# A recurrent mixer and an expert layer on one core: loads, tables and normalisation of the first block laid out anew

## The chip, the cores and the metric

The kernel runs on one NeuronCore of a Trainium2 chip. Five engines work side by side, each through its own queue in program order: PE (TensorE, matrix multiplication), DVE (VectorE), ACT (ScalarE), POOL (GpSimd) and SP (SyncE, which only issues DMAs here; ACT and POOL issue DMAs as well). [...]an instruction that waits holds up everything queued behind it on its engine. The metric is the device time of one execution in microseconds (us), lower is better.

## The reference

Two residual layers on x of shape (4, 1024, 256), float32. The first is a linear attention with decay over 16 heads of 16 channels; the second routes each token to two of eight experts, with a capacity for each expert. Cut to what matters here:

```python
x = x + attn(layernorm(x));  x = x + moe(layernorm(x))

# attn, for layer-normed x
xx = shift_by_one_token(x) - x                # the first token of a sequence has zero before it
k = (x + xx * maa_k) @ Wk.T                   # likewise r, v, and g = gelu(...)
w = exp(-exp(time_decay)); u = time_faaaa     # one number per head
Wmat[i, j] = w ** (i - j - 1) where i > j, u on the diagonal, 0 above
y     = (r @ k.T * Wmat) @ v + r @ state * w ** i
state = w ** Q * state + (k * w ** (Q - 1 - j)) @ v
out   = groupnorm_per_head(y) * ln_w + ln_b;  out = (out * g) @ Wo.T

# moe, for layer-normed x
the two largest of softmax(x @ gate_w.T), with a capacity of 320 per expert and sequence
final = sum over the two of prob * (silu(h @ w1) * (h @ w3)) @ w2
```

## The kernel before

**Tiling.** There are four sequences (b) of 1024 tokens, each cut into four blocks (blk) of 256 tokens, and each block into two chunks of 128. The recurrence is taken in chunks of Q = 128. x comes in eight loads of 512 tokens, that is of four tiles of 128, so that one load serves two blocks. `front` prepares a block: norm, transposition, the four mixed inputs, the projections r, k, v, g. `chunk` does the scores of a chunk, multiplies them with the decay tables, and updates the state; `back` does the head norm, the gate and the output projection; `route` the gate of the experts; `expert` one expert's three products. These are generators, and a loop written out by hand at the end of the kernel advances them turn by turn, block n's chunks beside block n+1's front. Experts are slotted in from block 6 on.

**Order.** The order of instructions on each engine comes from a scheduler that follows the program by priority and readiness. `tc.issue_after(ins)` holds the instructions of a `with` block behind ins, and `tc.keep_in_program_order(ins)` pins one to its place. Tiles of a pool with the same tag share `bufs` buffers in turn: the writer of a tile waits for the last reader of the tile that had the buffer.

**The start.** These are the names and lines that matter:

- `ch` (L101): 14 columns for each of 128 partitions, holding the eight mixing weights, ln_w, ln_b and the decays by channel. `hd` (L103): the decay and the bonus u of each head, 2 x 16 numbers spread to all partitions by the DMA. `wa` (L105): the five 256 x 256 weights in one load of 1280 KB. `gt` (L112): the gate; `lw` (L114): ln_w over all partitions. ACT issues all five. SP issues the first load of x (L97).
- `nlam` and `nlam_c` (L186 to L190): -exp(decay) by head and by channel: an exponential on ACT and a step on DVE each.
- `dist` (L194, L196): max(i - j - 1, 0), made on POOL and cut at zero on DVE.
- `wb`, `wk`, `ws` (L204 to L206): decay tables for the state and the keys, exponentials on ACT; `wsb` (L207) is ws spread over 128 columns by DVE.
- `wmat` (L209): 16 exponentials on ACT, one 128 x 128 table per head, then one `affine_select` on POOL (L211) that clears what is not strictly earlier, then `diagonals` (L218): 16 steps on DVE that add u on the diagonal.
- `centre_values` (L177 to L179): DVE takes the mean per head out of Wv's columns, giving `wvc`.
- `norm_stats` (L275 to L279): statistics of all four tiles of a load on DVE, with the reciprocal root by three Newton steps; `normed` (L285) applies them on ACT, tile by tile, into `xn`.
- In `front`: column 0 of `xT`, the last token of the block before (L303 for a sequence's first block, L305 on DVE for the others); the transposes `trx` (L310); their copy to `xT` on ACT (L313); `xx` on POOL (L315); `mixed` (L320), two steps on DVE for each of k, r, v; the projections `pc` (L330); v's product `pt` with wvc (L362); `kT` (L346), `rT` (L351), `rbT` (L352, needs wb), `vpad` (L367), the transposes `pk` (L376) and `kw` (L380, needs wk); g's mixed input `xm_g` on POOL (L387, L390). `xm` has two buffers.
- In `chunk`: the scores `pa` (L403), their product with wmat, `aw`, on DVE (L409), y (L426), `pu` (L436), and `state` on POOL (L450, needs wsb).
- `empty` (L815): a tile of zeros with token numbers, from which SP clears the experts' input `disp` in 32 stores (L240). The first eight go out as soon as empty is ready; then comes the load of the second half of sequence 0's x, a store to the output, and the other 24.

The start-up calls before, as the scheduler gets them: fronts(0); one step of the front; then `centre_values` behind the last step of the norm; the fill of `empty`; the clears; two more steps of the front; then all diagonals behind the same norm step.

On ACT that gives this order: the loads, the table of functions, nlam, nlam_c, the first tile's xn, wb (2), wk, ws, wmat (16), the second tile's xn, the copy of xT.

Of the kernel before, what the change touches and what calls it, by code (L numbers as in the profile page):

```python
# [8 lines left out]
F32 = mybir.dt.float32  # L9
I32 = mybir.dt.int32  # L10
# [39 lines left out]
def rwkv_then_moe_kernel(  # L50
# [4 lines left out]
    head: bass.AP,  # L55
# [39 lines left out]
    def load_x(b, r):  # L95
        t = keep.tile([P, RT, C], F32, tag="x", name=f"x{b}_{r}", bufs=4)
        nc.sync.dma_start(out=t, in_=rows(x, b, r))  # L97
        xb[b, r] = t

    ch = const.tile([P, 14], F32, tag="ch", name="ch")  # L100
    nc.scalar.dma_start(out=ch, in_=chan)  # L101
    hd = const.tile([P, 2, H], F32, tag="hd", name="hd")
    nc.scalar.dma_start(out=hd, in_=head.partition_broadcast(P))  # L103
    wa = const.tile([P, 5, CC, C], F32, tag="wa", name="wa")
    nc.scalar.dma_start(  # L105
        out=wa.rearrange("p w cc d -> p (w cc) d"),
        in_=w_attn.rearrange("(k p) d -> p k d", p=P),
    )
# [3 lines left out]
    nc.scalar.dma_start(out=gt[:, :, :E], in_=gate.rearrange("(cc p) e -> p cc e", p=P))  # L112
    lw = const.tile([P, C], F32, tag="lw", name="lw")
    nc.scalar.dma_start(out=lw, in_=lnw.partition_broadcast(P))  # L114

    load_x(0, 0)
# [47 lines left out]
    empty = fp.tile([P, 2, EK, W], F32, tag="w", name="empty", bufs=5)  # L164
# [8 lines left out]
    def centre_values():  # L173

        wv = wa[:, W_V, :, :].rearrange("p cc (h n) -> p (cc h) n", n=N)
        vmean = const.tile([P, CC * H], F32, tag="vmean", name="vmean")
        tc.keep_in_program_order(nc.vector.tensor_reduce(vmean, wv, AX.X, ALU.add))  # L177
# [15 lines left out]
    dist = a1.tile([P, P], F32, tag="xx", name="dist")  # L193
    nc.gpsimd.iota(dist, pattern=[[1, P]], base=-1, channel_multiplier=-1,  # L194
                   allow_small_or_imprecise_dtypes=True)
    nc.vector.tensor_scalar_max(dist, dist, 0.0)  # L196
# [6 lines left out]
    for cc in range(CC):  # L203
        nc.scalar.activation(wb[:, cc, :], col, AF.Exp, scale=nlam_c[:, cc:cc + 1])  # L204
    nc.scalar.activation(wk, nlam, AF.Exp, scale=back_)
    nc.scalar.activation(ws, nlam_c, AF.Exp, scale=float(P))  # L206
    nc.vector.tensor_copy(wsb, ws.unsqueeze(2).to_broadcast([P, CC, P]))  # L207
    for h in range(H):
        nc.scalar.activation(wmat[:, h, :], dist, AF.Exp, scale=nlam[:, h:h + 1])  # L209

    nc.gpsimd.affine_select(  # L211
        out=wmat, in_=wmat, pattern=[[0, H], [1, P]], compare_op=ALU.is_gt, fill=0.0,
        base=0, channel_multiplier=-1,
    )

    def diagonals():
        for h in range(H):
# [72 lines left out]
    def front(b, blk, o):  # L290
# [4 lines left out]
        if h0 == 0:  # L295
            last["stats"] = norm_stats(src, f"a{nm}")
# [631 lines left out]
```

## Time and profile before

| | us |
|---|---|
| median of three runs | 1138.74 |
| lowest, highest | 1132.3, 1141.37 |
| the profiled execution: its time | 1138.5 |
| the same: span from the first to the last instruction | 1136.8 |
| first load of x issued; first statistics of it | 0.82; 4.87 |
| load of wa issued; first use of it that waited | 1.84; 10.37 |
| first clear issued on SP | 22.18 |
| first scores of block 0 on PE | 30.83 |

The mean granted clock of TensorE was 0.982 of full speed. By stretches of the profile: between 0 and 20 us PE is busy for 1.3 us, between 20 and 40 for 15.0, between 40 and 100 for 57.1 of 60, between 100 and 200 for 85.0 of 100, at a mean granted clock of 0.89, and from 200 to 1000 for 97% of the time.

A busy PE is not a PE at its peak: the matmuls are pipelined and their ends are modelled. What can be read off surely is when an engine stood idle, and the profile names for each such stretch what ended it. The times are from one execution.

### The profile page before, as it was taken

What the parts mean: (1) busy time and instruction counts of PE and PEld (TensorE: products, weight loads), DVE (VectorE), ACT (ScalarE), POOL (GpSimd) and SP (SyncE); (2) the same over time, 40 slices, a digit from 0 to 9 for tenths busy, and PEclk for the clock granted to TensorE, in tenths of its full rate; (3) what the DMA queues carried; (4) which work ended last, traced back from release to release, by engine and by line L of the source; (5) the groups of instructions that cost most, each with busy time, mean ns of one, the idle gap of its engine ahead of it and who ended that gap; (6) DMA issues with size and microseconds to landing.
All of it is one profiled execution on the core that took longest, in us unless ns stands there. A gap on an engine that the chain in (4) does not pass through costs nothing. (4 is left out here: it accounts for less than half of the span.)

```text
span 1136.8 us, 15008 instructions
## 1 busy us (share of the span) xinstructions
PE 1061.6 (93%) x5640; PEld 799.2 (70%) x5640; DVE 509.6 (45%) x1577; ACT 280.9 (25%) x561; POOL 273.9 (24%) x262
## 2 busy tenths in 40 slices
PE   2889997999999999999999999989999999999996
PEld 2556564677776777687778677778888766666664
DVE  4678775555455455637552745322222222222221
ACT  4324251423142324412341321311111111111110
POOL 3222243122312331233133213312121111111111
PEclk9999996999999999999999999999999999999998
DMA  4992011143523352254316245456565644444421
GB/s 122 241 291 75 16 61 39 57 117 100 162 60 104 124 148 84 52 155 135 103 29 206 69 117 164 150 151 202 163 185 178 175 129 132 130 121 130 126 47 16
DMA packets 91564, 138.24 MB, mean 122 GB/s; under 512 B 5600, under 2 KB 73056, under 8 KB 91488
## 3 DMA queue, kind: packets, MB, share of 16 engines
q1 hardware_dynamic: 76048, 117.63, 33.1%
q0 software_dynamic: 13440, 18.13, 9.1%
q10 hardware_dynamic: 2000, 1.47, 0.4%
q8 instruction: 47, 0.77, 0.3%
q14 instruction: 29, 0.24, 0.1%
HBM read 103.52 MB, written 33.69 MB: 121 GB/s over the span
## 5 line engine op out<-in xcount | busy, mean ns | idle before, releaser
L732 PE MATMUL p<-xeT,w 128*128 128x256 f32 (+1 forms) x1792 | 448.4, 407 | 2.2 <-DVE xeT L723 1.1
L732 PEld LDWEIGHTS p<-xeT,w 128*128 128x128 f32 x1792 | 337.9, 190 | 100.7 <-ACT sl L737 5.7
L755 POOL DMA_INDIRECT y_out<-ye,xe x72 | 115.4, 1603 | 514.6 <-DVE ye L753 454.2
L749 PE MATMUL pw<-w,act 128*128 128x256 f32 x1008 | 231.0, 383 | 6.9 <-DVE ye L753 4.9
L739 DVE TENSOR_TENSOR act<-sl,p 128x256 f32<-128x256 f32 (+1 forms) x224 | 101.5, 453 | 282.2 <-PE p L732 267.4
L749 PEld LDWEIGHTS pw<-w,act 128*128 128x128 f32 x1008 | 188.0, 191 | 42.7 <-DVE ye L753 6.5
L737 ACT ACTIVATE sl<-p 128x256 f32<-128x256 f32 (+1 forms) x224 | 90.7, 410 | 497.5 <-PE p L732 477.7
L753 DVE TENSOR_SCALAR ye<-pw,xe 128x256 f32<-128x256 f32 x72 | 34.8, 483 | 173.3 <-PE pw L749 152.0
L409 DVE TENSOR_TENSOR aw<-pa,wmat 128x512 f32<-128x512 f32 x128 | 84.7, 684 | 59.9 <-PE pa L403 54.7
L403 PE MATMUL pa<-rT,kT 64*128 64x512 f32 x256 | 90.9, 654 | 1.1 <-DVE aw L409 1.1
L658 POOL DMA_INDIRECT disp<-hs,is x64 | 62.5, 977 | 115.5 <-DVE hs L655 62.8
L330 PE MATMUL pc<-xm,wa 128*128 128x256 f32 x256 | 68.5, 412 | 15.8 <-DVE xm L320 15.8
L330 PEld LDWEIGHTS pc<-xm,wa 128*128 128x128 f32 x256 | 49.6, 205 | 31.5 <-issue 17.7
L426 PE MATMUL y<-aw,vpad 128*32 128x128 f32 x1024 | 49.6, 286 | 1.6 <-DVE aw L409 1.6
L451 POOL TENSOR_TENSOR state<-state,upd 128x256 f32<-128x256 f32 x24 | 18.4, 766 | 126.2 <-DVE upd L441 75.3
L320 DVE SCALAR_TENSOR_TENSOR xm<-xx,ch,xT 128x256 f32<-128x256 f32 x96 | 43.6, 477 | 10.6 <-PE pc L330 5.8
L351 ACT ACTIVATE rT<-pc,par 128x512 f32<-128x512 f32 x64 | 38.7, 688 | 39.0 <-PE pc L330 37.5
L426 PEld LDWEIGHTS y<-aw,vpad 128*32 128x32 f32 x1024 | 27.4, 111 | 19.6 <-issue 8.0
L403 PEld LDWEIGHTS pa<-rT,kT 64*128 64x128 f32 x256 | 25.2, 188 | 22.5 <-issue 16.2
L346 ACT COPY kT<-pc 128x512 f32<-128x512 f32 x16 | 9.4, 586 | 106.8 <-PE pc L330 106.8
L362 PE MATMUL pt<-wvc,xm 128*128 128x256 f32 x128 | 32.7, 400 | 1.0 <-DVE aw L409 1.0
L501 PE MATMUL po<-wa,zT 128*128 128x256 f32 x128 | 31.7, 390 | 1.6 <-DVE zT L493 1.6
(163 smaller groups left out, 882.0 us busy)
## 6 DMA issues: line engine op xcount, KB each, us to landing
w<-w_in SPq DMA_DIRECT2D x96, 896.0 KB, 5.2
disp<-empty SPq DMA_DIRECT2D x24, 265.0 KB, 9.6
xe<-disp SPq DMA_DIRECT2D x24, 265.0 KB, 2.8
disp<-empty SPq DMA_DIRECT2D x8, 530.0 KB, 14.6
x<-x_in SPq DMA_DIRECT2D x8, 512.0 KB, 3.6
y_out<-x SPq DMA_DIRECT2D x8, 512.0 KB, 3.4
xe<-disp SPq DMA_DIRECT2D x8, 397.5 KB, 3.2
wa<-w_attn_in ACTq DMA_DIRECT2D x1, 1280.0 KB
```

Of the source, the lines that this page charges most:

```text
L320: nc.vector.scalar_tensor_tensor(xm[:, cc, :], xx[:, cc, :], maa(m, cc), xT[:, cc, 1:TB + 1], ALU.mult, ALU.add,)
L330: nc.tensor.matmul(pp[:, m * TB:(m + 1) * TB], wa[:, w, cc, m * P:(m + 1) * P], xm[:, cc, :], start=cc == 0, stop=cc == CC - 1,)
L351: nc.scalar.activation(o.rT[:, :, q, :], pp, AF.Copy, scale=par[:, q:q + 1])
L403: nc.tensor.matmul(pa, o.kT[rows64, cc, cols], o.rT[rows64, cc, :, cols], start=True, stop=True, tile_position=(64 * g, 0),)
L409: nc.vector.tensor_tensor(w.rearrange("p q i -> p (q i)"), pa, wmat[:, h0:h0 + 4, :].rearrange("p q i -> p (q i)"), ALU.mult,)
L426: nc.tensor.matmul(y[32 * g:32 * g + 32, :], o.vp[:, t, cc * 4 + g, q * 32:(q + 1) * 32], aw[cc, g // 2][:, (g % 2) * 2 + q, :], start=sta ...
L658: ins = nc.gpsimd.indirect_dma_start(out=disp[:, :], out_offset=bass.IndirectOffsetOnAxis(ap=idx_s[b, r][:, k, t:t + 1], axis=0), in_=hs[: ...
L732: nc.tensor.matmul(pp[:, :w], wt[:, cc, f * P:(f + 1) * P], xeT[:, cc, :w], start=cc == 0, stop=cc == CC - 1,)
L737: nc.scalar.activation(sl[:, :w], p1[:, :w], AF.Silu)
L739: nc.vector.tensor_tensor(act[:, :w], sl[:, :w], p3[:, :w], ALU.mult)
L749: nc.tensor.matmul(po[:, o:o + C], acts[f][:, t * P:(t + 1) * P], w2e[:, f, :], start=f == 0, stop=f == FC - 1,)
L755: ins = nc.gpsimd.indirect_dma_start(out=out[:, :], out_offset=bass.IndirectOffsetOnAxis(ap=xe.bitcast(I32)[:, t, C:C + 1], axis=0), in_=y ...
```

## The change: loads, halves of the tables, and the norm in two pairs of tiles

- **Host.** The two head tables are written out for all partitions and appended to `ch`, which grows from 14 to 46 columns; `hd` is now a view of it, and its own load is gone.
- **Loads.** ACT issues ch alone. SP issues the first load of x as two halves of two tiles, then the weights as five loads of 256 KB into five tiles, in the order k, r, v, g, o, then gt and lw.
- **Norm.** For sequence 0's first load the statistics are taken in two pairs of tiles; the second pair's steps are held behind the last step of the first. The two `normed` steps of block 0 are pinned in program order.
- **Tables.** wmat is made in two halves of eight heads: the first half's exponentials stand before the norm, the second half's, with the two affine_selects (one for each half), wb, wk, ws and wsb, behind the copy of block 0's xT. `dist`'s maximum and `wsb` go from DVE to POOL. The diagonals come behind block 0's last mixed input for v, and `centre_values` behind its first mixed input.
- **empty** becomes two tiles, each filled by itself.
- **xT's column 0** in the blocks that continue a sequence (12 of 16) is copied by ACT, not by DVE.

```diff
+    load_x(0, 0, TPB)
-    ch = const.tile([P, 14], F32, tag="ch", name="ch")
+    ch = const.tile([P, 14 + 2 * H], F32, tag="ch", name="ch")
     nc.scalar.dma_start(out=ch, in_=chan)
-    hd = const.tile([P, 2, H], F32, tag="hd", name="hd")
-    nc.scalar.dma_start(out=hd, in_=head.partition_broadcast(P))
-    wa = const.tile([P, 5, CC, C], F32, tag="wa", name="wa")
-    nc.scalar.dma_start(
-        out=wa.rearrange("p w cc d -> p (w cc) d"),
-        in_=w_attn.rearrange("(k p) d -> p k d", p=P),
-    )
+    hd = ch[:, 14:].rearrange("p (k h) -> p k h", k=2)
+    wa = [const.tile([P, CC, C], F32, tag=f"wa{w}", name=f"wa{w}") for w in range(5)]
+    w_rows = w_attn.rearrange("(k p) d -> p k d", p=P)
+    for w in (W_K, W_R, W_V, W_G, W_O):
+        nc.sync.dma_start(out=wa[w], in_=w_rows[:, w * CC:(w + 1) * CC, :])
...
-    nc.scalar.dma_start(out=lw, in_=lnw.partition_broadcast(P))
-    load_x(0, 0)
+    nc.sync.dma_start(out=lw, in_=lnw.partition_broadcast(P))
...
-    nc.vector.tensor_scalar_max(dist, dist, 0.0)
+    nc.gpsimd.tensor_scalar_max(dist, dist, 0.0)
...
+    def decay_of_heads(cc):
+        for h in range(cc * HC, (cc + 1) * HC):
+            nc.scalar.activation(wmat[:, h, :], dist, AF.Exp, scale=nlam[:, h:h + 1])
+
+    def only_earlier(cc):
+        hs_ = slice(cc * HC, (cc + 1) * HC)
+        nc.gpsimd.affine_select(
+            out=wmat[:, hs_, :], in_=wmat[:, hs_, :], pattern=[[0, HC], [1, P]],
+            compare_op=ALU.is_gt, fill=0.0, base=0, channel_multiplier=-1,
+        )
+
+    def decay_of_keys():
+        for cc in range(CC):
+            nc.scalar.activation(wb[:, cc, :], col, AF.Exp, scale=nlam_c[:, cc:cc + 1])
+        nc.scalar.activation(wk, nlam, AF.Exp, scale=back_)
+        nc.scalar.activation(ws, nlam_c, AF.Exp, scale=float(P))
+        nc.gpsimd.tensor_copy(wsb, ws.unsqueeze(2).to_broadcast([P, CC, P]))
...
-        if h0 == 0:
+        if b == 0 and r == 0:
+            if blk == 0:
+                last["stats"] = norm_stats(src, f"a{nm}", 0, TPB)
+                with tc.issue_after(last["nb"]):
+                    last["next"] = norm_stats(src, f"a{b}_1", TPB, TPB)
+            else:
+                last["stats"] = last["next"]
+        elif h0 == 0:
             last["stats"] = norm_stats(src, f"a{nm}")
...
-            nc.vector.tensor_copy(xT[:, :, 0:1], last["xT"][:, :, TB:TB + 1])
+            nc.scalar.copy(xT[:, :, 0:1], last["xT"][:, :, TB:TB + 1])
...
+    decay_of_heads(0)
     f, cur = fronts(0)
-    steps(f)
-    with tc.issue_after(last["nb"]):
+    steps(f, 2)
+    with tc.issue_after(last["xT_copy"]):
+        only_earlier(0)
+        decay_of_heads(1)
+        only_earlier(1)
+        decay_of_keys()
+    with tc.issue_after(last["xm"]):
         centre_values()
-    tc.keep_in_program_order(nc.gpsimd.memset(empty, 0.0))
     for i, base in enumerate(((B - 1) * T, 0)):
+        tc.keep_in_program_order(nc.gpsimd.memset(empty[i], 0.0))
...
     steps(f, 2)
-    with tc.issue_after(last["nb"]):
-        diagonals()
+    with tc.issue_after(last["xm"]):
+        for cc in range(CC):
+            diagonals(cc)
```

## The prediction, made before the changed kernel ran

> **What bounds the kernel now.** First the page: TensorE is busy for 93% of the span of 1136.8 us, so little more than its idle time can be won.
>
> ```profile
> PE 1061.6 (93%) x5640; PEld 799.2 (70%) x5640; DVE 509.6 (45%) x1577; ACT 280.9 (25%) x561; POOL 273.9 (24%) x262
> ```
>
> That leaves 75.2 us idle. The chain that ended last holds only the last scatter (0.1% of the span) and doesn't help. The waits of the first 30 us do: TensorE waited 17.0 us in all for xn on ACT. So I read the timeline of the first 60 us (columns: start, duration, engine, line, operation, tiles, count, idle time before it and its releaser).
>
> ```profile
> 9.23 0.60 ACT L285 ACTIVATE xn<-x,nba,rya 128x256 f32<-128x256 f32 x1 [2.74 <-DVE nba L279]
> ...
> 12.19 4.76 ACT L209 ACTIVATE wmat<-dist,nlam 128x128 f32<-128x128 f32 x16
> ...
> 16.86 0.58 ACT L285 ACTIVATE xn<-x,nba,rya 128x256 f32<-128x256 f32 x1
> ...
> 17.50 0.90 PE L310 MATMUL trx<-ident,xn 128*128 128x128 f32 x3 [7.07 <-ACT xn L285]
> ...
> 20.73 1.66 DVE L320 SCALAR_TENSOR_TENSOR xm<-xx,ch,xT 128x256 f32<-128x256 f32 x4
> ...
> 21.27 5.29 PE L330 MATMUL pc<-xm,wa 128*128 128x256 f32 x16 [2.87 <-DVE xm L320]
> ```
>
> ACT normalises one of the two x tiles, then does all sixteen decay tables, then the second tile. The transposes, xT, xx and xm wait behind that: the first projection starts at 21.27. The second hole comes soon after.
>
> ```profile
> 33.79 0.62 PE L426 MATMUL y<-aw,vpad 128*32 128x128 f32 x10
> 35.99 0.75 DVE L275 BATCH_NORM_STATS2 sta<-x 128x6 f32<-128x256 f32 x2 [2.72 <-DMA x<-x_in]
> ...
> 37.94 1.01 PE L330 MATMUL pc<-xm,wa 128*128 128x256 f32 x2 [3.53 <-DVE xm L320]
> ```
>
> The statistics of the second x load stand in VectorE's order in front of xm of block 1; the load, issued at 27.24 behind eight clears on SP, lands at 35.99, and TensorE idles 3.53 us. The stretches after it show a second price, the granted clock (sixth figure of the row, after the five engines):
>
> ```profile
> 39.00:40.00 1.00, 1.00 (x17) 0.58 (x17) 1.00 (x5) 0.00 (x0) 0.00 (x0) 0.50 1.07 218
> ...
> 41.00:42.00 1.00, 1.00 (x5) 0.74 (x3) 0.00 (x0) 0.00 (x0) 0.00 (x0) 0.73 1.08 230
> ```
>
> TensorE runs at half clock from about 38.4 to 41.5.
>
> **The change, part by part.** Until the first projection:
>
> - x in two halves, ahead of all else on SP. The first 512 KB took 4.05 us (issue 0.82, statistics 4.87); medians are 3.6 us for 512 KB (x) and 2.8 for 265 KB (xe), so a half saves 0.8 (bounds 0, and 2.0 for half of 4.05): statistics at 4.07. Two tiles take a 0.75 pair and a 0.30 pair: vea at about 5.1, not 6.65. From vea to the end of nb took 2.54: nb at 7.65. The nlam pair now stands inside this chain; its rows start 0.07 apart and fit in the 0.20 us steps: nothing. It would cost something only if ch landed after 5.5; before, ACT had both ch and hd by 6.18 at the latest.
> - ACT issues one load instead of five, so the function table's 1.28 us starts at 1.25, not 4.77. nlam is ready at 5.7; eight tables at 4.76/16 = 0.30 each end at 8.15, 0.5 after nb. The xn pair (1.09) ends at 9.25, against 17.44.
> - From the end of xn to the first projection took 3.83 us, of which 0.59 (20.14 to 20.73) was diagonals standing before xm. They now come after block 0's xm: 3.24 us, hence 12.5.
> - Against this, the second half's norm now stands on VectorE ahead of xm. Unhindered (statistics 1.05, then the 2.54 chain) it ends at 11.3, before xx at 11.95. But the trace has rows like these:
>
> ```profile
> 43.79 0.72 POOL L450 TENSOR_TENSOR state<-upd,wsb 128x256 f32<-128x256 f32 x1 [9.50 <-DVE upd L441]
> 43.83 0.70 DVE L277 TENSOR_SCALAR vea<-mva 128x4 f32<-128x4 f32 x1
> ...
> 45.12 1.04 POOL L387 TENSOR_TENSOR xm_g<-xx,ch 128x512 f32<-128x512 f32 x1 [0.61 <-PE pc L330]
> 45.17 1.00 DVE L264 TENSOR_TENSOR raa<-raa,rha 128x4 f32<-128x4 f32 x1
> ```
>
> A 0.17 us step lasts as long as the POOL instruction beside it. [...]It speaks against this change, which puts a chain of small VectorE steps beside the first affine_select (half of the 2.00 us that wmat's took at 17.02) and xx (1.04 at 19.10). A hold costs about the POOL instruction's length: the chain ends near 12.75, xm waits 0.8, the projection starts at 13.3. [...]I take 13.3, since these rows are the same steps. **Gain here: 21.27 - 13.3 = 8.0** (7 to 9.5).
>
> From there to the hole. VectorE: xm (2), vmean 0.69, xm (2), wvc 0.69, xm (2) end near 17, before TensorE needs them (5.29 us of projections: 18.6). Of the sixteen diagonals (0.27 each, from 3.50/13) six fit before xm_g at 18.6[...]; aw starts near 24.65, 0.65 later against the projection than before, covered by TensorE's transposes and scores until 25.85. The build's order then puts aw, both xm_1_0, aw and both xm_1_2 in front of the statistics, so block 1's projection no longer waits for the load: it starts at about 27.1. Before, 37.94 - 21.27 = 16.7; now 13.8: **2.9 more**. POOL's order: second affine_select to 14.1, wsb 0.6 (I take nearly state's 0.72; bounds 0.3 and 1.0), half memset 0.93, iota: the clears start at 15.9, not 22.18. The load lands 13.8 us after them as before, at 29.7; VectorE arrives at 29.15 and waits 0.6, while TensorE still has the rest of pc, pu and the next pc. No 3.5 us idle, no half clock: 1.65 us less, and I count **1.3**, leaving 0.35 for the reordered waits (0 to 1.65). At the second projection of block 1 the sum is 12.2.
>
> At nothing: five weight loads. [...]here the 1280 KB needed 8.5 us (issued 1.84, waited for until 10.37). Read as one load after the other at 2.8 us, x's halves first, W_K lands at 0.82 + 3 x 2.8 = 9.2, W_V at 14.8 and W_O at 20.4: vmean, due at 13.7, comes 1.1 late, and the xm and wvc behind it still stand before TensorE's need. By the rows, x and all the weights together were in by 10.4. The sum is the same by both. The gate and lw issues (1.2 us each) end on SP long before 15.9. dist's maximum on POOL (0.3) ends before 5.7. The twelve column copies on ACT (about 0.2 each) fall in ACT's idle time.
>
> After 50 us the order of TensorE's instructions is the same, and its waits there are for VectorE and POOL, which move along; weights and clears come earlier. So I carry 12: 1138.5 (the profiled execution: span 1136.8 and 1.7 around it, 0.24 under the median of 1138.74) - 12 = **1126.5**.
>
> **The rivals.**
>
> *The second hole stays.* The clears move up by only 6.3 us, the projection by 8. If ACT's second eight tables, which wb, wk and ws follow, or wsb bring the clears past 17.5, the load lands after 31.3, and xm_1_1 and the next aw behind it hold TensorE. For: 0.6 us of wait is already left. Against: some 6 us of TensorE work stands in front. Then only the start's 8 remain, less or more by a little: 1130.5.
>
> *The clock.* From 182 to 201 the granted clock stayed at 0.50 with TensorE busy for some 13 us, while the two other dips ended within 3.5. If it recovers as they did, some 5 us go as well: 1121.5. For: these dips follow idle stretches whose times shift. Against: the 4.1 us wait before it, for routing's running counts, is untouched.
>
> *Slower: the column copy at the head of ACT's queue.* xT's column 0 now waits on ACT for POOL's last reader of the buffer two blocks back, with kT and rT queued behind, and TensorE behind those. Twelve blocks: 1 us of wait each eats the gain, 2 us each give 1138.5 - 12 + 24 = 1150.5. Against: POOL's reader for block 3 ended at 47.33, and ACT gets there after xn at 58.3, 11 us later.
>
> *It doesn't separate.* x lands no earlier[...]: the start gains 6, the hole 1: 1131.5.
>
> **How the numbers follow.** Forecast 0.66 (its own range 1122.5 to 1129.5), second hole 0.18, clock 0.10, no separation 0.03, slower 0.03. A measurement here can tell about 1% from no change: 1127.4. Of the forecast about seven tenths lie below it, and the clock case: faster 0.57; slower 0.03; within 1% the rest, 0.40. The range 1120 to 1131.5 takes in the first three cases.
>
> **What would show it.** xn of both tiles together by about 9.3 on ACT; first pc at 12.5 to 13.5; one step of the second norm about 1 us long beside xx; first clear at about 16; no TensorE gap above 1.5 us between y and pc of block 1 and clock 1.00 there. Wrong if pc starts after 15, if statistics of the second load hold VectorE over 2 us, or if the kernels differ by 12 us at block 1's second projection and by under 8 at the end.

## The result, and the profile after

The changed kernel takes 1130.21 us (median of 8 runs, 1124.38 to 1135.49), the kernel before it in the same series 1135.32 (8 runs, 1131.92 to 1141.37): ratio 0.9936, 95% interval 0.9906 to 0.9965. In two later series, of 20 runs each, it stood at 0.9941 (0.9920 to 0.9963) and 0.9950 (0.9928 to 0.9972). So the change gains 0.5 to 0.65%, some 6 us, where 12 were forecast (1126.5 against 1138.5). The time lies inside the range, within 1% of the kernel before (to which 0.40 was given), and the forecast's own range (1122.5 to 1129.5) was missed by 0.7 us. That the time lies inside the range is owed in part to the base: in this series the kernel before took 1135.32 us, 3.2 us less than the 1138.5 from which the 12 were taken off.

The profiled execution took 1132.08 us with a span of 1129.9. TensorE's idle time fell from 75.2 to 64.0 us, 11.2 less, but its busy time rose from 1061.6 to 1065.9 with the same number of products. From the page:

```profile
PE 1065.9 (94%) x5640; PEld 802.1 (71%) x5640; DVE 510.8 (45%) x1577; ACT 282.8 (25%) x573; POOL 277.6 (25%) x266
```

More busy time for equal work means that products ran slower; the mean granted clock was 0.980 here and 0.982 before. That is the first sign of where part of the rest went: into the clock.

The start, from the timeline of the changed kernel (start, duration, engine, line, operation, tiles, count, idle time before it and its releaser):

```profile
8.32 1.08 ACT L293 ACTIVATE xn<-x,nba,rya 128x256 f32<-128x256 f32 x2
8.49 1.09 POOL L211 TENSOR_SCALAR_AFFINE_SELECT wmat<-wmat 128x1024 f32<-128x1024 f32 x1 [3.06 <-DVE sta L282]
8.68 0.93 DVE L284 TENSOR_SCALAR vea<-mva 128x2 f32<-128x2 f32 x1
...
11.06 1.04 POOL L334 TENSOR_TENSOR xx<-xT 128x512 f32<-128x512 f32 x1 [1.47 <-ACT xT L331]
...
11.18 0.95 DVE L148 TENSOR_SCALAR avg<-bd 128x8 f32<-128x8 f32 x1
...
12.61 0.16 DVE L286 SCALAR_TENSOR_TENSOR nba<-mva,rya 128x2 f32<-128x2 f32 x1
12.71 0.88 DVE L339 SCALAR_TENSOR_TENSOR xm<-xx,ch,xT 128x256 f32<-128x256 f32 x2
...
13.25 1.22 PE L349 MATMUL pc<-xm,wa 128*128 128x256 f32 x2 [2.90 <-DVE xm L339]
```

Both tiles are normalised in one pair that ends at 9.40, and the first projection starts at 13.25 instead of 21.27. Two VectorE steps that take 0.16 to 0.17 us in the profile of before (vea at 6.65, avg at 11.18) take 0.93 and 0.95, each beside a GpSimd instruction of about that length (1.09 and 1.04): the two holds that the prediction counted. The second of them fell on the constant avg, not on a step of the norm; but it stands in front of the norm's last steps and moves them just the same.

From there to block 1, the same timeline:

```profile
14.70 5.23 PE L349 MATMUL pc<-xm,wa 128*128 128x256 f32 x13
16.27 5.02 SPq L247 DMA_DIRECT2D disp<-empty  x8
17.87 3.75 DVE L225 SCALAR_TENSOR_TENSOR wmat<-ident,ch,wmat 128x128 f32<-128x128 f32 x14
20.01 2.52 POOL L406 TENSOR_TENSOR xm_g<-xx,ch 128x512 f32<-128x512 f32 x1 [2.83 <-PE pc L349]
22.61 1.09 POOL L409 TENSOR_TENSOR xm_g<-xm_g,xT 128x512 f32<-128x512 f32 x1
...
23.75 1.99 PE L349 MATMUL pc<-xm_g,wa 128*128 128x256 f32 x8 [1.67 <-POOL xm_g L409]
...
29.71 0.70 PE L349 MATMUL pc<-xm,wa 128*128 128x256 f32 x2 [0.45 <-DVE xm L339]
...
31.36 0.74 DVE L282 BATCH_NORM_STATS2 sta<-x 128x6 f32<-128x256 f32 x2
...
33.30 1.89 PE L349 MATMUL pc<-xm,wa 128*128 128x256 f32 x8
```

The 3.53 us hole in front of block 1's first projection is 0.45, and the statistics of the second x load no longer wait for a DMA: the clears started at 16.27, before TensorE could run out. But the first two projections end at 19.93, 6.68 us after their start (before: 5.29), and GpSimd's first xm_g, 1.04 us before, lasts 2.52 beside VectorE's fourteen diagonals and ends 0.9 us after the last of them: they hold it. TensorE waits 1.67 us for it. Block 1's second projection is at 33.30 instead of 43.08: 9.8 us won, of 12.2 predicted.

Further on I follow the end of each block's k projection by its copy on ACT (kT, start in us):

| kT of block | before | changed | gain |
|---|---|---|---|
| 0 | 24.87 | 17.07 | 7.8 |
| 1 | 42.29 | 32.51 | 9.8 |
| 2 | 63.00 | 52.95 | 10.1 |
| 3 | 85.98 | 75.84 | 10.1 |
| 4 | 110.67 | 105.29 | 5.4 |
| 8 | 244.94 | 239.44 | 5.5 |

Five microseconds go in one piece between blocks 3 and 4. The windows of the changed kernel there (busy us of PE, PEld, DVE, ACT, POOL, then the granted clock, the DMA share and GB/s):

```profile
90.00:94.00 4.00, 2.79 (x8) 0.67 (x4) 3.94 (x22) 2.79 (x6) 0.10 (x1) 1.00 0.02 4
94.00:96.00 2.00, 1.77 (x9) 1.78 (x10) 0.40 (x1) 0.66 (x2) 0.00 (x0) 0.59 0.40 87
96.00:98.00 2.00, 2.00 (x23) 1.60 (x21) 1.22 (x5) 1.46 (x3) 0.79 (x1) 0.50 0.50 176
...
104.00:106.00 2.00, 2.00 (x14) 1.77 (x13) 0.71 (x2) 0.71 (x2) 0.00 (x0) 0.85 0.00 0
```

For 10.2 us TensorE runs at half clock. Before, the same work shows the same idle time and no loss:

```profile
100.00:102.00 2.00, 1.81 (x6) 0.50 (x6) 1.97 (x19) 0.79 (x2) 0.24 (x1) 1.00 0.00 0
102.00:104.00 2.00, 1.12 (x2) 0.29 (x2) 1.98 (x5) 2.00 (x5) 0.00 (x0) 1.00 0.00 0
104.00:106.00 2.00, 1.64 (x14) 1.54 (x14) 0.72 (x2) 1.06 (x3) 0.00 (x0) 1.00 0.40 71
```

### The profile page after: what moved, and what is told of

Same layout as the page of the kernel before. It is cut to its first block, busy times and chain, and to the rows that moved or that the text cites. A ratio compares the mean times of both kernels' runs of the same rounds, so it can differ in the third digit from the quotient of the medians.

```text
span 1129.9 us, 15009 instructions
## 1 busy us (share of the span) xinstructions
PE 1065.9 (94%) x5640; PEld 802.1 (71%) x5640; DVE 510.8 (45%) x1577; ACT 282.8 (25%) x573; POOL 277.6 (25%) x266
## 5 line engine op out<-in xcount | busy, mean ns | idle before, releaser
L349 PE MATMUL pc<-xm,wa 128*128 128x256 f32 x256 | 70.2, 420 | 12.7 <-DVE xm L339 12.7
L422 PEld LDWEIGHTS pa<-rT,kT 64*128 64x128 f32 x256 | 25.4, 189 | 22.9 <-issue 16.6
## 6 DMA issues: line engine op xcount, KB each, us to landing
disp<-empty SPq DMA_DIRECT2D x8, 530.0 KB, 12.9
```

The source lines that it names most:

```text
L349: nc.tensor.matmul(pp[:, m * TB:(m + 1) * TB], wa[w][:, cc, m * P:(m + 1) * P], xm[:, cc, :], start=cc == 0, stop=cc == CC - 1,)
L422: nc.tensor.matmul(pa, o.kT[rows64, cc, cols], o.rT[rows64, cc, :, cols], start=True, stop=True, tile_position=(64 * g, 0),)
```

## The experiments

Theory A: the start gains what was predicted, and the rest is lost to stretches of half clock that fall by chance where TensorE has idled a little. Theory B, the rival: something in the changed order loses it, each time in the same place. In the end both hold, each at a place of its own. Four runs went with one series (kernel before: 1138.56 us), four with a second (1140.63), four with a third (1133.47), which ran on another chip; a time is to be read against the kernel before of its own series. A ratio compares the single runs of the two kernels and is not the quotient of the medians.

**The changed kernel again.** No edit.

> The changed kernel, nothing altered. In its first trace block 3's kT copy came 10.1 us earlier than before the change and block 4's only 5.4 us; between them TensorE ran at half clock from 94.8 to 104.6 us after an idle stretch that the kernel before has as well. Theory A (the clock dips fall by chance): kT of blocks 0 to 3 at 17.1, 32.5, 53.0 and 75.8 again within 0.5, and the dip near 95 us absent or of another length, so that block 4's kT is 5 to 10 us ahead of the 110.67 before. Theory B (something in the change takes 5 us back at that place): block 4's kT again 5 to 5.7 us ahead.

1131.14 us, ratio 0.9941. Its profile:

```profile
13.16 5.37 PE L349 MATMUL pc<-xm,wa 128*128 128x256 f32 x16 [2.90 <-DVE xm L339]
17.64 5.45 DVE L225 SCALAR_TENSOR_TENSOR wmat<-ident,ch,wmat 128x128 f32<-128x128 f32 x14
18.62 1.05 POOL L406 TENSOR_TENSOR xm_g<-xx,ch 128x512 f32<-128x512 f32 x1 [1.54 <-PE pc L349]
...
20.90 1.99 PE L349 MATMUL pc<-xm_g,wa 128*128 128x256 f32 x8 [0.21 <-POOL xm_g L409]
```

Here xm_g is not held (now the diagonals are: 5.45 us for what took 3.75), and block 1's second projection starts at 30.67, 12.4 us before that of the kernel before. So the start does not repeat within the 0.5 us that were expected: kT of blocks 1 to 3 stands at 29.88, 50.33 and 77.57. No half clock stands at 94 to 104, and kT of block 4 is 8.2 us ahead, as A says.

But 6.8 us of half clock stand at 71 to 78, where kT's gain falls from 12.7 at block 2 to 8.4 at block 3, and here TensorE waits first. SP issues the load of x for the next sequence behind the 24 clears; VectorE waits for it, and aw stands behind VectorE's statistics of it:

```profile
54.63 3.85 SPq L98 DMA_DIRECT2D x<-x_in  x2
...
66.69 0.43 DVE L282 BATCH_NORM_STATS2 sta<-x 128x6 f32<-128x256 f32 x1 [3.98 <-DMA x<-x_in]
...
68.75 1.26 DVE L428 TENSOR_TENSOR aw<-pa,wmat 128x512 f32<-128x512 f32 x2
...
69.47 1.12 PE L422 MATMUL pa<-rT,kT 64*128 64x512 f32 x2 [0.74 <-DVE aw L428]
```

The same statistics in the kernel before, and in the changed kernel's first profile:

```profile
76.66 0.43 DVE L275 BATCH_NORM_STATS2 sta<-x 128x6 f32<-128x256 f32 x1 [1.26 <-DMA x<-x_in]
```

```profile
65.47 0.43 DVE L282 BATCH_NORM_STATS2 sta<-x 128x6 f32<-128x256 f32 x1
```

The load landed 10 us earlier than before the change, VectorE came for it 12.7 us earlier. All profiles are compared at this place below, under "The load of the next sequence".

**Only ACT's order.** The kernel before, with all decay tables behind the copy of xT (`dist` also gets a buffer of its own; two lines of the edit):

```diff
+    with tc.issue_after(last["xT_copy"]):
+        tables()
```

> The kernel before with one part of the change: all decay tables, with their selection and wb, wk, ws, go behind block 0's copy of xT; loads, norm, halves and empty as before. Theory A (the start's gain is the order on ACT): the xn pair starts at 9.2 as in the kernel before and ends at 10.3, the first projection at about 13.7, that is 7.5 of the 8.0 us; aw of block 0 waits for the tables (16 of them end near 17.5), the clears come near 22 or later, and the whole gains 3 to 6 us. Theory B (the loads and the split norm carry it): the first projection after 17 and a gain under 2 us.

1145.34 us, ratio 1.0092 (1.0056 to 1.0129): slower, though 3 to 6 us of gain were expected.

```profile
13.38 6.94 PE L332 MATMUL pc<-xm,wa 128*128 128x256 f32 x16 [2.32 <-DVE xm L322]
20.46 1.04 POOL L389 TENSOR_TENSOR xm_g<-xx,ch 128x512 f32<-128x512 f32 x1 [7.65 <-PE pc L332]
21.45 2.00 POOL L212 TENSOR_SCALAR_AFFINE_SELECT wmat<-wmat 128x2048 f32<-128x2048 f32 x1
...
24.36 4.85 DVE L219 SCALAR_TENSOR_TENSOR wmat<-ident,hd,wmat 128x128 f32<-128x128 f32 x15
25.23 1.21 POOL L392 TENSOR_TENSOR xm_g<-xm_g,xT 128x512 f32<-128x512 f32 x1
26.49 3.62 PE L332 MATMUL pc<-xm_g,wa 128*128 128x256 f32 x8 [2.53 <-POOL xm_g L392]
```

The projection starts at 13.38, so nearly the whole 8 us of the start comes from ACT's order alone. The other parts add 0.1 at this place: they bring the start of xn forward by 0.7 (9.02 here, 8.32 in the changed kernel), and the second norm, which they put in front of xm, takes 0.6 of it back. But the tables end late: the mask of 2.00 us and the fill of empty (1.86) stand between the two steps of xm_g, TensorE waits 2.53 us, half clock follows (3.4 us at 26 to 30), and the clears start only at 26.55. At kT of block 1 it is 6.5 us ahead of the kernel before, not the 7.6 to 12.4 of the profiles with the whole change. Between blocks 2 and 3 it loses 8.6 us more than the kernel before: the load of the next sequence stands behind the late clears, VectorE waits 6.86 us for it, TensorE 4.49 for VectorE, and 10.2 us of half clock follow. At block 3 it is 2.2 us behind. Its runs have the lowest mean clock of the series, 0.972.

**No diagonals** (the bonus u is left out of the output):

```diff
-    with tc.issue_after(last["xm"]):
-        for cc in range(CC):
-            diagonals(cc)
```

> The changed kernel without the sixteen diagonal steps: the bonus u is left out of the computation. Theory A (the diagonals on VectorE hold POOL's xm_g[...]): xm_g's first step takes 1.04 us, not 2.52, TensorE waits under 0.5 us for xm_g, not 1.67, and the first scores start at about 24.2, not 25.68. Theory B (xm_g is slow for another reason, such as its own semaphores or the clears' transfers): 2.5 us again and the scores at 25.7. Over the whole 1 to 2 us faster than the changed kernel under A, the same under B.

xm_g takes 1.04 us at 18.74, block 1's second projection stands at 30.62 as in the first rerun, and the whole takes 1131.12 us, ratio 0.9950 (0.9924 to 0.9975), no less than the kernel with diagonals. Taking away what holds xm_g wins nothing that can be measured at the end, though 1 to 2 us were expected. The profile shows where it goes: kT is 12.5 us ahead at block 1 and 8.6 at block 3, for here too VectorE waits for the next sequence's x (3.90 us). That the diagonals hold xm_g is not shown by this run (xm_g became ready at 18.74, and in two profiles with diagonals it passed them at 18.62 and 18.81) but by the rows in which it ends 0.9 us after the last of them.

**A warm start.** Twenty products without use ahead of the first transposes and twelve behind them, to see whether the first projections then run faster.

```diff
+            spin = bank("f", "spin")
+            for _ in range(20):
+                tc.keep_in_program_order(nc.tensor.matmul(
+                    spin[:, :P], ones, ident, start=True, stop=True, skip_group_check=True))
```

> The changed kernel with 32 idle products of constants on TensorE, 20 before block 0's transposes and 12 after them, into a PSUM bank that nobody reads. Theory A (the first two projections are slow because TensorE's clock is still low): the sixteen matmuls take 3.8 to 4.5 us, not 6.67, and everything after moves up by 2 to 3 us (the first scores at about 23). Theory B (they wait for operands): 6.7 us again, and no gain.

1132.66 us, ratio 0.9970 (0.9936 to 1.0004).

```profile
14.46 3.29 PE L358 MATMUL pc<-xm,wa 128*128 128x256 f32 x14 [0.53 <-DVE xm L348]
17.19 3.75 DVE L225 SCALAR_TENSOR_TENSOR wmat<-ident,ch,wmat 128x128 f32<-128x128 f32 x14
17.83 4.01 POOL L415 TENSOR_TENSOR xm_g<-xx,ch 128x512 f32<-128x512 f32 x1 [0.91 <-PE pc L358]
...
23.07 2.48 PE L358 MATMUL pc<-xm_g,wa 128*128 128x256 f32 x8 [3.16 <-POOL xm_g L418]
```

The two projections took 4.5 us from 13.23 on, a wait of 0.53 among them, instead of 5.4 to 6.7: sixteen products at full clock take 3.78 (two rows of 1.89 further on). The trace has its first entry of the granted clock at 7.4 us here, and at 16.5 to 19.3 in the profiles with 5.4 to 6.7. So 0.9 to 2.2 us of the start go with the time of that entry. The time won ran into the diagonals: xm_g came ready early, was held for 4.01 us, TensorE waited 3.16, and 3.4 us of half clock followed at 24 to 28. The first scores start at 25.47 instead of 25.68, not at 23 as A had it.

**The kernel before again.** No edit, one profile.

> The kernel before, unchanged, one more profile. In the first profile it had half clock at 38.4 to 41.5 and none from there to 135, and the changed kernel's two profiles each had one stretch of half clock of 8 to 10 us between 70 and 105. Theory A (the stretches fall by chance[...]): this profile may show one between 60 and 115 as well, and its time is then above 1138.5; with or without it the sum of half clock over the span is 38 to 46 us. Theory B (the order of the changed kernel brings the stretch between 70 and 105, that of before does not): again none between 45 and 130. A single profile cannot refute A; a stretch there refutes B. Span 1132 to 1142.

1146.82 us with a span of 1145.1, above the 1132 to 1142 expected; half clock sums up to 50.7 us, above A's 38 to 46. Its waits around 103 us and its windows:

```profile
103.02 1.12 PE L403 MATMUL pa<-rT,kT 64*128 64x512 f32 x2 [0.88 <-DVE aw L409]
104.70 0.48 PE L310 MATMUL trx<-ident,xn 128*128 128x128 f32 x1 [0.56 <-ACT xn L285]
```

```profile
100.00:104.00 4.00, 3.12 (x10) 0.97 (x8) 3.97 (x21) 2.52 (x5) 0.57 (x1) 1.00 0.01 4
104.00:106.00 2.00, 1.44 (x8) 1.31 (x8) 0.85 (x2) 1.13 (x3) 0.00 (x0) 0.63 0.30 38
...
118.00:120.00 2.00, 2.00 (x12) 1.71 (x11) 0.81 (x2) 0.08 (x1) 0.83 (x1) 0.96 0.01 4
```

The waits, 0.88 and 0.56 us, are the ones of the changed kernel's first profile, and the half clock follows them here too, for 13.6 us. In the first profile of this same program it did not. For the stretch at 94 to 104, theory B needs it to belong to the changed order; it doesn't.

**Half of the diagonals behind kw.**

```diff
-        for cc in range(CC):
-            diagonals(cc)
+        diagonals(0)
+    with tc.issue_after(last["kw"]):
+        diagonals(1)
```

> The changed kernel with the diagonals of heads 8 to 15 held back behind kw, so that at most eight stand on VectorE when GpSimd's first xm_g becomes ready at 18.6. Theory A (whichever of the diagonals and xm_g starts first holds the other; in the first profile of the changed kernel the diagonals held xm_g to 2.52 us and TensorE waited 1.67 us for it): xm_g takes 1.03 to 1.2 us, pc_g follows by 21.1 with under 0.4 us of wait, the first scores by 23.0, the second projection of block 1 by 30.9, but the later diagonals put aw of heads 8 to 15 a little later. Whole 1129 to 1131, since half of the profiles of the changed kernel have it so already; scatter smaller. Theory B (the second half of the diagonals behind kw comes in front of aw and costs what it saves): first scores the same, but block 1's second projection at 31.5 or later, whole equal or up to 1 us slower.

1141.74 us, ratio 0.9983 (0.9953 to 1.0013). xm_g took 1.55 us at 19.40, not 1.03 to 1.2, and the second projection of block 1 stood at 31.78: between A and B. This series has no run of the changed kernel to set it against; by the ratios nothing is won (0.9983 against 0.9936 to 0.9950). The expected 1129 to 1131 was written for a series with the kernel before at 1138.56.

**Filled waits.** Products without use in TensorE's two longest waits, for the second routing's running counts and for block 7's xm; 34 and 38 of them, then 17 and 18:

```diff
+            if w == W_K:
+                idle(pp, FILL.get(b * BPS + blk, 0))
...
+        if (b, r) == (0, 1):
+            idle(pc, 17)
```

> The changed kernel with 34 products without use on TensorE in front of the running counts of the second routing (where TensorE waited 4.13 us at 170 to 174) and 38 in front of the first projection of block 7 (4.78 us at 184 to 189); at full clock one takes 0.10 to 0.11 us, so they fill the waits and lengthen the path by 0 to 1.5 us. Theory A (half clock from 175 to 197 is what these idle waits bring): no half clock from 170 to 200, 15 to 19 us of half clock less in the span, so the end is 6 to 9 us earlier at best and 4 or more after what the products cost; whole 1122 to 1127, and mean clock 0.985 to 0.990. Theory B (the half clock there has another cause, or it comes back elsewhere as the stretch at 38 did): mean clock within 0.002 of 0.981 and the whole within 2 us of the changed kernel.

1141.90 us, ratio 1.0023. Half clock between 170 and 200 was gone (0 against 13.7 to 20.5 us in the others), but I had costed a product at 0.11 us where it stands in the trace as two records and takes 0.23: the products took 7.8 and 9.4 us. So, with half of them:

> The changed kernel with 17 products without use in front of the running counts of the second routing and 18 in front of the first projection of block 7, half of what the run before had. There each took 0.23 us with its two passes and so 7.8 and about 10 us against waits of 4.1 and 4.8 us: some 8 us too much, while half clock from 173 to 194 (17.0 us in the control, 8.5 us of lost time) was gone. Theory A (half clock is the price of these waits): 3.9 and 4.1 us of products fit into the waits, no half clock from 170 to 197, from kT of block 6 to kT of block 7 29 to 32 us where the control has 36.6, and at equal time before it 4 to 7 us less at the end; ratio to before 0.988 to 0.991. Theory B (VectorE's chain of the routing sets this stretch, TensorE's clock only follows): the stretch from kT of block 6 to block 7 stays above 34.5 us and the whole within 2 us of the changed kernel.

1127.87 us, ratio 0.9964 (0.9944 to 0.9984), not better than the control of its series. First this kernel's waits, then those of the control:

```profile
175.25 3.96 PE L302 MATMUL pcnt<-ident,ones 128*128 128x128 f32 x34
179.77 0.41 PE L640 MATMUL pcnt<-before,ones 128*128 128x40 f32 x2 [0.57 <-DVE before L631]
184.16 4.29 PE L302 MATMUL pc<-ident,ones 128*128 128x128 f32 x36
194.51 3.78 PE L358 MATMUL pc<-xm,wa 128*128 128x256 f32 x8 [6.07 <-DVE xm L346]
```

```profile
181.40 0.65 PE L629 MATMUL pcnt<-before,ones 128*128 128x40 f32 x2 [4.13 <-DVE before L622]
196.14 3.75 PE L349 MATMUL pc<-xm,wa 128*128 128x256 f32 x8 [4.71 <-DVE xm L339]
```

With the products the clock stayed up until 192 (half clock 6.8 us instead of 17.1), and block 7's projection did not come sooner: from kT of block 6 to it 33.4 us, in the control 32.8. VectorE sets the time of xm (TensorE waits 6.07 us for it here, 4.71 in the control), and a higher clock brought it no sooner. B, as written for this run, holds: the stretch from kT to kT stayed at 37.2 us.

**The norm of the second half later**, behind the first xm, and the first half of the tables behind the copy of xT too:

```diff
-                with tc.issue_after(last["nb"]):
-                    last["next"] = norm_stats(src, f"a{b}_1", TPB, TPB)
...
+        last["next"] = norm_stats(xb[0, 0], "a0_1", TPB, TPB)
```

> The changed kernel with the norm of the second pair of tiles moved behind the first projection's xm on VectorE, and the first half of the decay tables behind the copy of xT too. Theory A (as the prediction counts it: eight tables end 0.5 us after nb and the second norm[...] ends 0.8 us behind xx): xn by 8.9, xx by 11.5 and the first projection at 11.9 to 12.4, 0.9 to 1.4 us earlier than 13.2; tables, first decay mask and the clears come 2 to 3 us later, the clears at 18 to 19, so the load of block 1's second half lands 2 us later and holds VectorE up to 1.5 us; whole within 1.5 us of the changed kernel. Theory B (the first projection's start is all that counts): whole 1 us or more faster than the changed kernel, 1129.5 or less.

The projection starts at 12.17, 1.08 us sooner. Of this 0.5 is xn, which starts at 7.80 instead of 8.32 because no table stands in front of it, and 0.6 is xm, which follows xx at once; the prediction had priced the two holds at 0.8. The rest goes the other way: the clears start at 22.71, the second load holds VectorE for 2.76 us, and the load of the next sequence, behind the later clears, for 12.00, so that TensorE waits 8.76 us. Between blocks 2 and 3 alone it loses 12.9 us more than the kernel before. The whole takes 1147.58 us, ratio 1.0022 (0.9993 to 1.0051), by the ratios more than the 1.5 us behind the changed kernel that A allowed.

**Control.** The changed kernel in the third series.

> The changed kernel once more, as the control of this call. In the first two calls it stood 5.1 and 7.4 us under the kernel before by medians and 7.8 us at equal granted clock; theory A (12 us gained by block 1, 4 to 5 us of it lost to stretches of half clock that before's first profile didn't have) expects ratio 0.991 to 0.997 again, in its profile kT of block 1 at 29.5 to 33, half clock in pieces of 3.4 us each, and one or more of them between 70 and 115. Theory B (the gain at block 1 is lost in the order of later work): kT of block 4 less than 7 us ahead of 110.67 though no half clock stands before it.

1129.56 us, ratio 0.9950. First projection 13.25, xm_g not held, block 1's second projection 30.86; half clock at 71 to 79 (6.8 us) and at 98 to 109 (10.2 us), and of kT's gain of 12.5 at block 2 there remain 6.5 at block 3, 1.9 at block 4 and 1.4 at block 8. So 11 us were lost by block 8, where A had 4 to 5. The first piece has the wait for the load in front of it again, longer than in the rerun:

```profile
68.92 0.43 DVE L282 BATCH_NORM_STATS2 sta<-x 128x6 f32<-128x256 f32 x1 [6.03 <-DMA x<-x_in]
...
71.70 2.07 PE L422 MATMUL pa<-rT,kT 64*128 64x512 f32 x2 [2.79 <-DVE aw L428]
```

The span is 9.2 us shorter than that of the first profile of before, so 7.8 come back after block 8. They can't be put down to the change: from kT of block 8 to the end the four profiles of the third series, on their chip, take 882.6 to 884.1 us, the ten others 887.0 (the rerun) to 891.9 (the first profile of before); the second profile of before takes 888.4.

**One load for the projection weights**, behind the halves of x:

```diff
-    for w in (W_K, W_R, W_V, W_G, W_O):
-        nc.sync.dma_start(out=wa[w], in_=w_rows[:, w * CC:(w + 1) * CC, :])
+    nc.sync.dma_start(
+        out=wa5.rearrange("p w cc d -> p (w cc) d"),
+        in_=w_attn.rearrange("(k p) d -> p k d", p=P),
+    )
```

> The changed kernel with the projection weights as one load of 1280 KB on the same queue, behind the halves of x, in place of five of 256 KB. Theory A (as the prediction costs it, nothing: all weights were in by 10.4 us before, and the first projection starts at 13.2): first projection at 13.0 to 13.5, x statistics at 3.8 to 4.1, ratio to before within 0.002 of the control. Theory B (five loads bring W_K early enough and one does not): the first projection waits for wa and starts at 14 or later, whole 1 us or more slower than the control.

First projection 13.15, x statistics 3.94, ratio 0.9957 (0.9936 to 0.9977): as the control. Five loads are worth nothing here.

**Column copies on VectorE again.**

```diff
-            nc.scalar.copy(xT[:, :, 0:1], last["xT"][:, :, TB:TB + 1])
+            nc.vector.tensor_copy(xT[:, :, 0:1], last["xT"][:, :, TB:TB + 1])
```

> The changed kernel with the copy of xT's column 0 on VectorE, as in the kernel before, in place of ACT. Theory A (prediction: twelve copies of 0.2 us in ACT's idle time cost nothing, and none waits at the head of ACT's queue): equal to the control within 1.5 us. Theory B (the slower rival: on ACT the copy waits for GpSimd's last reader with kT and rT behind it): 2 to 12 us faster than the control, and in the control's profile a wait of ACT for GpSimd of 0.3 us or more in front of these copies.

1129.62 us, ratio 0.9971 (0.9950 to 0.9991), the control's interval overlapping: no gain from taking them off ACT. On VectorE they take 307 ns each. The row of these copies in the groups by line, in the control (busy, mean ns, idle time before):

```profile
L323 ACT COPY xT<-xT 128x2 f32<-128x2 f32 x12 | 2.2, 187 | 0.3
```

On ACT all twelve together wait 0.3 us. The mechanism of the slower rival isn't there.

**The load of the next sequence.** All fourteen profiles, at the place where the rerun lost its 4 us: when SP issues the load of x for the second sequence, how long VectorE waits for it, how long TensorE then waits for aw, the half clock that begins there, and the time from kT of block 2 to kT of block 3 (us):

| profiles | issued | VectorE waits | TensorE waits | half clock | kT to kT |
|---|---|---|---|---|---|
| before, both | 63.4, 63.0 | 1.26, 0.54 | no | none | 23.0 |
| changed (first), warm start | 53.4, 52.9 | under 0.2 | no | none | 22.9 |
| filled by half, columns on VectorE | 55.6, 56.4 | 2.68, 2.43 | no | none | 23.4, 23.2 |
| rerun, control, no diagonals, split, filled waits, one load | 54.3 to 56.1 | 3.90 to 6.03 | 0.66 to 2.79 | 6.8 | 27.2 to 29.0 |
| only ACT's order | 64.3 | 6.86 | 4.49 | 10.2 | 31.6 |
| norm later | 64.5 | 12.00 | 8.76 | 13.7 | 35.9 |

Where VectorE waits 3.9 us or more, TensorE runs out of work and half clock follows, in all eight profiles; where it waits less, neither happens, in all six. The last two rows have the start early and the clears late, and lose most. So this stretch is not a matter of chance alone: the compute in front of it moved forward further than the load. Of the 4 to 6 us that the fourth row loses, 0.2 to 2.0 are longer waits of TensorE and some 4 are longer busy time. While VectorE waits, the DMA engines are busy throughout (in the control a share of 1.06 at 389 GB/s from 66 to 71 us), so the load's place behind the clears may not be all that delays it. No run issued it ahead of them; what that would win is not shown.

**What a stretch of half clock costs** depends on where it falls. Further on the time from one kT to the next in the profiles, with the half clock in between:

| from kT to kT | half clock | us |
|---|---|---|
| block 3 to 4 | none (before, rerun, no diagonals, split, one load, columns on VectorE) | 24.7 to 25.1 |
| block 3 to 4 | 10.2 us (changed, control, warm, filled by half) | 29.2 to 29.5 |
| block 6 to 7 | 20.5 us (before) | 37.1 |
| block 6 to 7 | 17 us (changed, rerun, control) | 36.6 |
| block 6 to 7 | 6.8 us (filled by half) | 37.2 |

Between blocks 3 and 4, where TensorE's own waits are the same in all profiles (0.88 and 0.56 us), 10.2 us of half clock cost about 4.5; between 6 and 7, where VectorE's chain is the bound, 17 cost nothing.

## Why the prediction was right and wrong

**The start: right.** 8.0 us predicted, 8.0 measured (21.27 to 13.25), and part by part: xn's pair by 9.25, measured 9.40; the second norm's end 12.75, measured 12.77; first clear 15.9, measured 16.27. That the first projection is hit to 0.05 us is luck: xx ended 0.15 later than forecast, and the two holds cost 0.6 behind it instead of 0.8. The first projection started at 13.15 to 13.29 in all profiles that keep the order.

**From there to the hole: right in mechanism, too large by a term that varies.** The hole is gone, and block 1 waits for no load, in every profile of the changed kernel. Of the 12.2 us at block 1's second projection seven profiles with this order show 12.4 and 12.2 (rerun, control), 9.9 (one load), 9.8 (the first; filled waits), 8.1 (filled by half) and 7.6 (columns on VectorE), 10.0 on average. The term that was mis-sized is "six fit before xm_g at 18.6": the prediction let xm_g's two steps (1.04 and 1.09 us before, 2.13 together) hold the diagonals every time. They did in the rerun and the control, where xm_g came ready at 18.62 and 18.81; in the five others (19.22 to 20.01) the diagonals ran on, and xm_g lasted 2.5 to 3.3 us; in two of these half clock at 24 to 28 followed.

What feeds it is the other term, "5.29 us of projections": in the seven it was 5.4 to 6.7. The products start 0.43 us apart at first, and 0.22 apart from the moment at which the trace has its first entry of the granted clock (before it the column reads 1.00). That moment is 24.5 in the first profile of before, 16.5 in the rerun, 16.8 in the control, and 17.6 to 19.3 in the five others; the later it is, the later xm_g comes to the diagonals, without exception. With the warm start it is 7.4, and the projections take 4.5. So 5.29 was a draw of the clock too.

**"After 50 us ... its waits there are for VectorE and POOL, which move along; weights and clears come earlier. So I carry 12": wrong, and this is the step that missed the time.** Two things do not move along. The first is a load: VectorE's wait at block 2 is for the next sequence's x, which SP issues behind the 24 clears. Before, it landed at 76.66 and cost TensorE nothing. In the six profiles with the early start in which TensorE waited for it, it landed at 66.5 to 69.6, 7 to 10 us earlier, where kT of block 2 is 10 to 13 us ahead. That the clears come earlier was counted, by how much was not. It is the prediction's own rival, the second hole, one load further on. In the seven profiles kT's gain at block 3 is 5.6 to 10.1 us, 7.4 on average.

The second is the clock between blocks 3 and 4. Four of the seven profiles have 10.2 us of half clock there, about 4.5 us of time each, after waits that are the same in all; before has 13.6 us there in one of its two profiles. The profile from which the prediction started, at 1138.5, had been spared. The dip at 38 to 41, on the other hand, stands in both profiles of before and in none of the changed kernel, as predicted.

The prediction's own test, 12 at block 1 and under 8 at the end, can't be read from single profiles: the spans differ from the first profile of before by 13.3 (rerun), 9.2 (control) and 6.9 us (first), and the medians of the series by 7.4, 3.9 and 5.1. At block 8 the three were 8.4, 1.4 and 5.5 us ahead.

**How much of the 12 is the kernel's and how much the draw.** Each run lists its mean granted clock. Within a series, with one slope for all kernels, 0.001 of clock goes with 1.05 us (first series) and 0.95 us (third), and the scatter about the line is 1.4 and 1.2 us (standard deviation) where each kernel's runs scatter by 2.7 to 5.0. At equal clock (0.981) the changed kernel is 7.8 us faster in the first series (1130.5 against 1138.3) and 7.6 in the third (1126.6 against 1134.2). Its clock was lower there, 0.9807 against 0.9815 and 0.9787 against 0.9816, and that takes about 1 and 3 us of it back. The profiles give nearly the same sum: 12.2 forecast, 10.0 at block 1 after the hold of xm_g, 7.4 at block 3 after the load. That the two agree so well is not a proof, since the waits for the load bring half clock of their own, which equal clock takes out. It does explain why the kernel without diagonals, at 1130.2 by equal clock, was hardly faster than with them: what the hold did not take, the load did.

**The rivals.** The second hole did not stay where it was, but came again one load later. The clock of 182 to 201 did not recover, and filling it showed that its 5 us were not there to win: that rival priced half clock at half of the busy time, in a stretch that VectorE sets. The ACT copies cost nothing, and x did land earlier (statistics at 3.84; before 4.87).

**At nothing**: five loads, gate and lw issues, column copies: held, the first and the last by a run of their own.

## What to carry to other kernels

A gain at the start of a kernel arrives further on only if everything that the later work waits for moves along by as much. Before carrying it, look for the transfers that stand behind something that moves less (here a load of x behind 24 clears on one queue), and set the time at which each lands against the time at which it will be wanted. Waits of 0.88 and 0.56 us brought 10.2 us of half clock in some profiles here, at about 4.5 us, more than the waits themselves, and in others none. So take several profiles of the kernel before, not one, and look in them for stretches of half clock, and for the wait in front of each, before calling any of them chance, cause or effect; read their price from the spacing of a landmark with and without them, not from their length. And when an order is changed, ask what comes free at the same moment on VectorE and GpSimd: here xm_g and the diagonals, pushed together, held each other (xm_g took 2.52 to 4.01 us instead of 1.04, or the fourteen diagonals 5.45 instead of 3.75), and which one lost changed from run to run.

## What the runs showed of the hardware

Half clock comes in pieces: in the first 300 us of the fourteen profiles the stretches lasted 3.4, 6.8, 10.2, 13.6 or 20.5 us, and within each profile all changes of the clock lie whole multiples of 3.413 us apart. On this grid it can be seen when the two waits between blocks 3 and 4, 0.88 and 0.56 us with 1.12 us of products between them, bring half clock. In five profiles both waits fall into one step of the grid, with 1.26 to 1.44 us of idle time in it, and half clock starts at the end of that step each time (changed, control, warm, filled by half, and the second of before). In six an edge of the grid lies 0.3 us or more behind the end of the first wait, so that no step has more than 0.88 us, and none follows. In the last three (only ACT's order, filled waits, norm later) the edge lies within 0.06 us of the end of the first wait, and half clock starts one step later; why is open.

In the second profile of before 1.26 us of idle time in one step of 3.413 us were followed by half clock. Busy time did not end it at once: in the changed kernel's first profile half clock stood for 10.2 us, from 94.3 to 104.6, while TensorE was busy throughout after the first two microseconds (2.00 of 2.00 in every window from 96 to 106, of which two are shown above). What ends it, no run here tells.

The holds between VectorE and GpSimd went in both directions: GpSimd's xm_g, 1.04 us without the diagonals, lasted up to 4.01 us beside VectorE's back-to-back diagonals (warm start), longer than any single one of them (one every 0.26 us). In the six profiles in which all fourteen ran through, it ended 0.9 us after the last of them. In two (rerun, control) it got in between after the fourth and took 1.05 us, and the fourteen lasted 5.45 and 5.46 us instead of 3.75. There it had become ready 0.19 us after the start of a diagonal, in the six at 0.01 to 0.12 or 0.22 to 0.24; whether that decides it is open.
